# Preparing a selective scan by halves, in another PSUM bank and at another place of a four-layer decoder

## The chip, the cores and the metric

The kernel runs on one core of one Trainium2 chip. The metric is the device time of one execution in microseconds (us). Several executions of the same program are timed, and the median counts. One more execution is recorded by the hardware profiler; all durations of single instructions come from that one.

## The reference, cut to what matters

A decoder of four layers works on `x` of shape (4, 256, 256): 4 sequences of 256 tokens with 256 features. Each layer has an attention, a cross part that takes a context `ctx_1024` of shape (4, 256, 128), and a feed-forward part, each added to `x` and followed by a layer norm. The change touches the first five parts:

- layer 0 attention: 16 query heads of 128 features over one shared key and value head, causal;
- layer 0 cross part: a selective scan over the context, gated by `x`;
- layer 0 feed-forward, the "thought": the last token of each sequence is normed, projected, and put through four rounds of a small network; the result is broadcast to all tokens under a sigmoid gate;
- layer 1 attention: 16 heads of 16 features;
- layer 1 cross part: the same selective scan with other weights.

The scan, with 256 channels `e`, 16 states `n` and 256 positions per sequence:

```python
u = silu(conv4(in_proj_w @ ctx) + conv_b)        # 4 taps along the positions
dt_lo, B, C = split(x_proj_w @ u)                # 8, 16, 16 rows
delta = softplus(dt_proj_w @ dt_lo + dt_proj_b)
state = state * exp(delta * A) + delta * u * B   # one position after the other, A = -exp(A_log)
y = sum_n(state * C) + D * u
out = y * silu(x)
```

`u`, `delta`, `B` and `C` depend on the context alone, not on `x`. So the scan's result is needed only at the gate, after the attention of the same layer.

The thought:

```python
t = norm(x)[:, -1] @ agg
for _ in range(4):
    t = t + gelu(norm(t) @ d1 + d1_b) @ d2 + d2_b
x = norm(x + sigmoid(x @ gate_w + gate_b) * (t @ bc_w + bc_b))
```

## The kernel before, in words

All 1024 tokens stay on the chip: `x` as 8 tiles of 128 tokens, and `xT`, its transpose. The program is emitted in Python and handed to a scheduler that puts the instructions of each engine in an order before the run: an instruction that was emitted earlier has the higher priority, and one emitted later is taken where the engine would stand idle by the scheduler's own clock. [...] Emission order is therefore a priority and not the final order, and a buffer that comes free early lets later work move ahead.

**Scans.** The class `Scans` (from line 398) holds the selective scan. `begin(pre)` starts a generator `_steps`: it first emits the whole preparation for all four sequences and stops. Then each `next` emits one scan, which is one state `n` of one sequence `b`, 64 in a layer. `beside(n)` calls it n times and `upto(b)` until sequence b is done. One scan consists of:

- a DMA on SP that reads rows B and C back from DRAM (`bcd`) to all partitions into a tile `bc` (4 buffers);
- two exponentials on ACT into `dA` (3 tiles), one for each half of the channels;
- a product on POOL, `s = du * B` (4 buffers);
- on DVE the scan itself over 512 columns and the product with C;
- on PE the addition of `s` to the sum over the states, a product with the identity into the PSUM bank `ssmps`. Sequence b keeps that bank from n = 0 to n = 15; there is one such bank.

The preparation uses the same bank for everything: four convolutions of four products each, taps `tap` times context, evicted to `u` on ACT; then for each half of the tokens the product `xp`, whose rows go through `xd` to DRAM, and two products `dt`. Softplus is built from Abs, Exp and Ln on ACT and a sum on DVE (`delta`), and `du = delta * u` is formed on POOL. [...] a change of table is an instruction of its own, ACT_TABLE_LOAD.

**First attention**, `run_mqa` (line 232): 32 items, eight for each sequence, each of four heads and 128 tokens. Item n turns its shares, and beside it the scores of item n + 1, the queries of item n + 4 (in the bank `pm`, tag "mm", one buffer) and two scans are emitted. `gate_pair` for a finished sequence is emitted at the third item of a later sequence. After the last item come the last gate and the preparation of the second layer's scans, `begin("l1x")`.

**Thought**, `run_thought` (line 585): it first centres its weights, then computes the gate (8 tiles, 16 products, one sigmoid over 2048 columns), then takes the last tokens (`last`, `tok`), norms and projects them, and goes through four rounds (`sq`, `var`, `rstd`, `tT`, `h`, `hT`, `add`). After the rounds 24 scans are emitted, and then `gated` and `added` for each sequence, which form the new `x` and its transpose.

**Second attention**, `run_gqa` (line 982) with `SmallHeads`: one scan is emitted beside each of the 8 projections and each of the 32 steps of the heads. `heads16.then` calls `gate_pair` for a sequence whose projection is done. The mixture of experts follows.

Lines 111 (tensor_tensor), 115, 117, 120, 123 (POOL), 126 (ACT) and 132 (PE) are helpers, so in the profile many different operations share one of these lines; the tile's name tells them apart.

Of the kernel before, what the change touches and what calls it, by code (L numbers as in the profile page):

```python
# [19 lines left out]
F32 = mybir.dt.float32  # L20
# [4 lines left out]
AF = mybir.ActivationFunctionType  # L25
# [6 lines left out]
P = 128  # L32
B, L, D = 4, 256, 256
NT = B * L // P
# [197 lines left out]
def run_mqa(K, w, more):  # L232
    nc, tc = K.nc, K.tc
    with ExitStack() as ctx:
# [120 lines left out]
                    K.add_out(2 * b + k, acc[b][:, k, :], not K.fused(0))  # L355

        N = 8 * B
        keys(0)
        queries(0)
        K.scans.begin("l0x")  # L360
# [7 lines left out]
        for n in range(N):  # L368
            shares(n)
            if n + 1 < N:  # L370
                scores(n + 1)
            if n + 4 < N:
                queries(n + 4)
            if n in (2, 3, 4, 5):
                rest.pop(0)()
            if n == 6:
                more()
            K.scans.beside(2)
            turn(n)
            if n:  # L380
                output(n - 1)
            sums(n)
            if n % 8 == 2 and n > 8 and K.fused(0):
                gate_pair(K, wk, y, n // 8 - 1)
        output(N - 1)
        if K.fused(0):
            gate_pair(K, wk, y, B - 1)
            K.scans.begin("l1x")

# [8 lines left out]
class Scans:  # L398
    def __init__(self, K, ctx):
        tc = K.tc  # L400
        self.K = K
        self.one = ctx.enter_context(tc.tile_pool(name="ssm1", bufs=1))
        self.wk = ctx.enter_context(tc.tile_pool(name="ssm2", bufs=4))
        self.ps = ctx.enter_context(tc.tile_pool(name="ssmp", bufs=1, space=PSUM))
        self.dram = ctx.enter_context(tc.tile_pool(name="ssmd", bufs=2, space=bass.MemoryType.DRAM))

        self.dA = [self.one.tile([P, DC, L], F32, name=f"dA{k}") for k in range(3)]
        for t in self.dA:
            K.nc.gpsimd.memset(t[:, :, 0:1], 0.0)
        self.w = {}  # L410
        self.left = iter(())
        self.done = 0

    def load(self, pre):
        K = self.K
# [9 lines left out]

    def begin(self, pre):

        self.left = self._steps(pre)
        self.done = 0
        next(self.left)  # L430

    def beside(self, n):

# [5 lines left out]
        while self.done <= b:  # L439
            next(self.left, None)  # L440

    def _steps(self, pre):
        K, nc, w, wk = self.K, self.K.nc, self.w[pre], self.wk
        cols = w["cols"]
        N = B * L
        u = self.one.tile([P, DC, N], F32, name="u", bufs=2)
        delta = self.one.tile([P, DC, N], F32, name="delta")
        du = self.one.tile([P, DC, N], F32, name="du")


        taps = []
        for j in range(4):
            t = wk.tile([P, D], F32, name="tap", tag="bc", padded_shape=[P, 2 * L])
            nc.sync.dma_start(out=t, in_=K.A[f"{pre}_cw"][:, j * D : (j + 1) * D].to_broadcast([P, D]))
            K.ptt(t, t, w["in"], MUL)
            taps.append(t)
        for h in range(2):
            for c in range(DC):
                ps = self.bank()
                for j in range(4):  # L460
                    K.mm(ps, taps[j][:, c * P : (c + 1) * P], K.ctxp[:, 2 * h : 2 * h + 2, j : j + L], j == 0, j == 3)
                K.act(u[:, c, 512 * h : 512 * h + 512], ps, AF.Identity, bias=cols[:, c, 0:1])
        K.act(u, u, AF.Silu)
        negA = self.one.tile([P, DC, 16], F32, name="negA")
        K.act(negA, cols[:, :, 2:18], AF.Exp)
        K.ts(negA, negA, -1.0, None, MUL)
        bc = self.dram.tile([2, 16, N], F32, name="bcd")
        for h in range(2):
            s = slice(512 * h, 512 * h + 512)
            xd = wk.tile([P, 512], F32, name="xd", tag="s")  # L470
            ps = self.bank()
            for c in range(DC):
                K.mm(ps[0:40, :], w["xp"][:, c, :], u[:, c, s], c == 0, c == DC - 1)
            nc.scalar.copy(xd[0:40, :], ps[0:40, :])
            for k in range(2):
                nc.sync.dma_start(out=bc[k, :, s], in_=xd[8 + 16 * k : 24 + 16 * k, :])
            for c in range(DC):
                ps = self.bank()
                K.mm(ps, w["dt"][:, c * P : (c + 1) * P], xd[0:8, :])

                K.ts(delta[:, c, s], ps, cols[:, c, 1:2], None, ADD)
                K.act(du[:, c, s], ps, AF.Abs, bias=cols[:, c, 1:2])
        K.act(du, du, AF.Exp, scale=-1.0)
        K.act(du, du, AF.Ln, bias=K.eps[1.0])
        for c in range(DC):
            K.stt(delta[:, c, :], delta[:, c, :], 0.0, du[:, c, :], MAX, ADD)
            K.ptt(du[:, c, :], delta[:, c, :], u[:, c, :], MUL)

        turn = 0
        self.y = u  # L490

        late = []
        bank = {}

        def add(b, n, s):
            if n == 0:
                bank[b] = self.bank()
            y = bank[b]
            K.mm(y, K.ident, s.rearrange("p c l -> p (c l)"), n == 0, n == 15)
            if n == 15:  # L500
                for c in range(DC):
                    v = u[:, c, b * L : (b + 1) * L]
                    K.stt(v, v, cols[:, c, 18:19], y[:, c * L : (c + 1) * L], MUL, ADD)
                self.done += 1

        for b in range(B):
            lo = b * L
            for n in range(16):
                yield
                if len(late) > 1:  # L510
                    add(*late.pop(0))
                t = wk.tile([P, 2, L], F32, name="bc", tag="bc")
                nc.sync.dma_start(out=t, in_=bc[:, n, lo : lo + L].unsqueeze(0).to_broadcast([P, 2, L]))
# [14 lines left out]
                K.tt(s, s, again(t[:, 1, :], DC), MUL)  # L528
                late.append((b, n, s))
        for t in late:  # L530
            add(*t)


def gate_pair(K, pool, y, b):

    K.scans.upto(b)
    gate = pool.tile([P, DC, L], F32, name="gate")

    K.act(gate, K.x[:, 2 * b : 2 * b + 2, :], AF.Silu)
# [45 lines left out]
def run_thought(K, w, more):  # L585
# [4 lines left out]
    with ExitStack() as ctx:  # L590
# [79 lines left out]
        cb = one.tile([P, DC], F32, name="cb")  # L670
        nc.vector.tensor_copy(cb, centred(d2b.unsqueeze(2), 1)[:, :, 0])


        gate = one.tile([P, NT, D], F32, name="gate")
        for i in range(NT):
            ps = pm.tile([P, D], F32, name="ps", tag="mm")
            for c in range(DC):
                K.mm(ps, K.xT[:, c, i * P : (i + 1) * P], w["gate"][:, c, :], c == 0, c == DC - 1)
            K.tt(gate[:, i, :], ps, row["gate_b"], ADD)
# [15 lines left out]
        th = one.tile([P, DC, B], F32, name="th")  # L695
        K.tt(th, ps, wide(w["cols"][:, 0, :], B), ADD)
        ct = centred(th, B)

        K.stt(th, wide(d2b, B), 4.0, th, MUL, ADD)
        last = spare.tile([P, B], F32, name="last")  # L700
# [281 lines left out]
def run_gqa(K, w, more):  # L982
    nc, tc = K.nc, K.tc
    more()
    with ExitStack() as ctx:
# [1452 lines left out]
```

## Time and profile before

| | us |
|---|---|
| median of three runs | 2520.05 |
| lowest, highest run | 2504.77, 2521.07 |
| the profiled execution | 2505.99 |
| its span, first to last instruction | 2504.2 |
| mean granted PE clock | 0.939 |
| PE, PEld, DVE, ACT, POOL busy | 2277.2, 1526.3, 1460.8, 802.4, 530.6 |

How to read it: PE is the matrix engine and PEld its weight loads, DVE the vector engine, ACT the scalar engine, POOL the GpSimd, SP the queue that issues DMAs. A float32 product appears as two records[...]. Busy time of PE is modelled and slightly long. Times in the profile count from the first instruction. By the names in the trace the stages end at about 391 us (last item of the first attention), 566 (thought) and 798 (second attention).

### The profile page before, as it was taken

The page shows a single profiled execution, that of the slowest core. Times are in us where ns is not written, and L with a number is a line of the kernel's source. Part 1 is how long each engine was busy: PE and PEld are TensorE (multiplying, and loading weights), DVE is VectorE, ACT ScalarE, POOL GpSimd, SP SyncE. Part 2 cuts the span into 40 slices and gives each one's busy share as a digit, 9 for nine tenths or more (in the row PEclk, how much of TensorE's full clock was granted, in tenths as well). Part 3 has the DMA queues.
Part 4 walks back from the last instruction along what each step waited for, and adds up shares of the span by engine and source line. Part 5 has one row for each costly group of instructions (what it writes and reads, how often), then busy time and mean ns, then how long its engine had stood idle before and what let it go on. Part 6 is the DMA issues. An engine that isn't in the chain of part 4 may idle for free. (4 is left out here: it accounts for less than half of the span.)

```text
span 2504.2 us, 28859 instructions
## 1 busy us (share of the span) xinstructions
PE 2277.2 (91%) x10624; PEld 1526.3 (61%) x10624; DVE 1460.8 (58%) x2824; ACT 802.4 (32%) x1781; POOL 530.6 (21%) x617
## 2 busy tenths in 40 slices
PE   8798988648996999989999999999999989799997
PEld 5466654224443565545888888888776544476774
DVE  3798984588875412182356454444555667774556
ACT  3566663422442111153111111111122244343434
POOL 2544543663332222210001100011110002100001
PEclk9899999677987999999999999999988899999999
DMA  5221221122223254230123111211100002100000
GB/s 197 60 60 45 57 54 40 41 61 42 52 46 109 88 158 130 66 112 29 45 66 110 48 58 45 71 46 47 46 22 1 20 18 70 40 1 1 1 1 17
DMA packets 132836, 138.99 MB, mean 56 GB/s; under 512 B 13876, under 2 KB 120726, under 8 KB 130904
## 3 DMA queue, kind: packets, MB, share of 16 engines
q1 hardware_dynamic: 132696, 137.16, 19.1%
q8 instruction: 84, 1.38, 0.2%
q14 instruction: 56, 0.46, 0.1%
HBM read 134.27 MB, written 2.85 MB: 55 GB/s over the span
## 5 line engine op out<-in xcount | busy, mean ns | idle before, releaser
L132 PE MATMUL ps<-xw,xcT 128*128 128x256 f32 (+1 forms) x2304 | 519.0, 382 | 0.3 <-ACT YT L126 0.3
L132 PEld LDWEIGHTS ps<-xw,xcT 128*128 128x128 f32 x2304 | 430.7, 190 | 64.2 <-issue 1.9
L132 PE MATMUL sc<-kT,qT 32*128 32x256 f32 (+2 forms) x1024 | 240.7, 412 | 11.1 <-DVE qn L129 10.7
L520 DVE TENSOR_TENSOR_SCAN s<-dA,s 128x512 f32<-128x512 f32 x128 | 210.3, 1666 | 35.6 <-POOL s L123 35.4
L123 POOL TENSOR_TENSOR s<-du,bc 128x512 f32<-128x512 f32 x128 | 178.9, 1410 | 231.0 <-PE ssmps L132 191.1
L132 PEld LDWEIGHTS sc<-kT,qT 128*128 128x128 f32 (+1 forms) x1024 | 152.9, 206 | 92.3 <-issue 57.8
L132 PE MATMUL ssmps<-s,idz 128*128 128x512 f32 x256 | 147.1, 683 | 33.6 <-DVE s L111 33.5
L111 DVE TENSOR_TENSOR xp<-ps,xb 128x256 f32<-128x256 f32 x96 | 40.4, 421 | 227.0 <-PE ps L132 224.8
L126 ACT ACTIVATE dA<-delta,negA 128x255 f32<-128x255 f32 x256 | 117.7, 501 | 160.5 <-DVE s L520 160.3
L126 ACT ACTIVATE p<-sc,nm 128x256 f32<-128x256 f32 (+1 forms) x256 | 112.1, 445 | 109.5 <-DVE nm L129 103.7
L111 DVE TENSOR_TENSOR hT<-u,a 128x512 f32<-128x512 f32 x48 | 33.2, 691 | 186.1 <-PE u L132 186.1
L132 PE MATMUL o<-pT,vt 128*128 128x256 f32 (+1 forms) x352 | 121.1, 467 | 21.9 <-ACT pT L332 21.5
L123 POOL TENSOR_TENSOR xp<-xp,rn 128x128 f32<-128x128 f32 x96 | 35.2, 402 | 476.9 <-DVE rn L1406 476.9
L169 POOL TENSOR_SCALAR rstd<-mv 128x2 f32<-128x2 f32 x48 | 12.2, 255 | 551.3 <-DVE mv L161 541.4
L126 ACT ACTIVATE sq<-xp 128x1024 f32<-128x1024 f32 x24 | 25.4, 1057 | 314.3 <-DVE xp L111 314.2
L129 DVE TENSOR_REDUCE qn<-sc 128x2 f32<-128x480 f32 (+1 forms) x192 | 87.2, 506 | 43.6 <-PE sc L132 42.9
L129 DVE TENSOR_REDUCE nm<-sc 128x2 f32<-128x512 f32 (+1 forms) x128 | 77.2, 613 | 49.8 <-PE sc L132 49.2
L126 ACT ACTIVATE e<-sT 128x512 f32<-128x512 f32 x128 | 70.1, 591 | 108.3 <-PE sT L132 107.8
L1474 DVE TENSOR_TENSOR_SCAN dec<-xT,idz 128x256 f32<-128x256 f32 (+1 forms) x192 | 89.8, 537 | 25.0 <-DMA xT<-ad 25.0
L111 DVE TENSOR_TENSOR s<-s,bc 128x512 f32<-128x512 f32 x128 | 103.6, 829 | 1.1
L123 POOL TENSOR_TENSOR hT<-hT,sel 128x512 f32<-128x512 f32 x48 | 60.7, 1268 | 202.1 <-DVE hT L111 102.6
L132 PE MATMUL sT<-q,kT 32*128 32x256 f32 (+1 forms) x384 | 96.4, 502 | 1.7 <-ACT e L126 1.5
(503 smaller groups left out, 4067.1 us busy)
## 6 DMA issues: line engine op xcount, KB each, us to landing
bc<-bcd SPq DMA_DIRECT2D x128, 256.0 KB, 4.6
xw<-in_l2a_xw_dram SPq DMA_DIRECT2D x24, 768.0 KB, 4.9
xT<-ad SPq DMA_DIRECT2D x12, 1024.0 KB, 4.5
wj<-in_l1f_gate_dram SPq DMA_DIRECT2D x48, 128.0 KB, 2.6
wj<-in_l1f_up_dram SPq DMA_DIRECT2D x48, 128.0 KB, 3.1
wj<-in_l1f_down_dram SPq DMA_DIRECT2D x48, 128.0 KB, 3.5
sel<-cwd SPq DMA_DIRECT2D x32, 192.0 KB, 3.0
sel<-cwd SPq DMA_DIRECT2D x32, 128.0 KB, 3.5
```

Source lines behind the costliest of these rows:

```text
L111: self.nc.vector.tensor_tensor(out=out, in0=a, in1=b, op=op)
L123: self.nc.gpsimd.tensor_tensor(out=out, in0=a, in1=b, op=op)
L126: self.nc.scalar.activation(out, in_, func, **kw)
L129: self.nc.vector.tensor_reduce(out=out, in_=in_, axis=AX.X, op=op, **kw)
L132: self.nc.tensor.matmul(out, lhsT=lhsT, rhs=rhs, start=start, stop=stop)
L169: self.nc.gpsimd.tensor_scalar(out=out, in0=in_, scalar1=add, scalar2=None, op0=ADD)
L520: nc.vector.tensor_tensor_scan(out=s.rearrange("p c l -> p (c l)"), data0=dA.rearrange("p c l -> p (c l)"), data1=s.rearrange("p c l -> p ...
L1474: nc.vector.tensor_tensor_scan(out=dec[:, k, h, :], data0=ap[:, h, at(bb, k, j) : at(bb, k, 2)], data1=K.idz[:, 0 : (2 - j) * P], initial=0.0,
```

## The change: what it does

- `begin` is split into `prepare(pre, bank)`, a generator that emits the preparation into banks that the caller hands in, and `start(pre)`, which sets up the scans. `start` no longer takes the generator's first `next`, so the first call of `beside` counts one step that emits no scan.
- The preparation goes by halves of two sequences: `u`, `delta` and `du` are tiles of one half with three buffers each (before: whole tiles, `u` with two buffers, the others with one). Within a half it runs from the convolutions to `du`. Silu reads PSUM directly. The taps have tiles of their own. `du` is formed on DVE.
- For the second layer it is emitted behind the last gate of the first attention as before, now with products into `pm`, the bank of the queries, and eight scans are emitted right after it.
- Gates of the first attention are emitted three items later, and `gate_pair` no longer calls `upto` itself; its callers do, or have emitted enough.
- In the thought the last tokens' path comes ahead of the gate's 16 products, and 32 scans are emitted in place of 24.

```diff
@@ run_mqa
+        bank = lambda: pm.tile([P, 512], F32, name="ps", tag="mm")
...
-            if n % 8 == 2 and n > 8 and K.fused(0):
-                gate_pair(K, wk, y, n // 8 - 1)
+            if K.fused(0):
+                if n % 8 == 5 and n > 8:
+                    gate_pair(K, wk, y, n // 8 - 1)
         output(N - 1)
         if K.fused(0):
+            K.scans.upto(B - 1)
             gate_pair(K, wk, y, B - 1)
-            K.scans.begin("l1x")
+            for _ in K.scans.prepare("l1x", bank):
+                pass
+            K.scans.start("l1x")
+            K.scans.beside(8)
@@ class Scans
     def begin(self, pre):
-        self.left = self._steps(pre)
+        for _ in self.prepare(pre, self.bank):
+            pass
+        self.start(pre)
+
+    def start(self, pre):
+        self.left = self._steps(*self.ready[pre])
+        halves = self.ready[pre][1]
+        self.y = lambda b: halves[b // 2][0][:, :, b % 2 * L : b % 2 * L + L]
         self.done = 0
-        next(self.left)
...
-    def _steps(self, pre):
+    def prepare(self, pre, bank):
...
-        u = self.one.tile([P, DC, N], F32, name="u", bufs=2)
-        delta = self.one.tile([P, DC, N], F32, name="delta")
-        du = self.one.tile([P, DC, N], F32, name="du")
...
-            t = wk.tile([P, D], F32, name="tap", tag="bc", padded_shape=[P, 2 * L])
+            t = self.one.tile([P, D], F32, name=f"tap{j}")
...
         for h in range(2):
+            u, delta, du = (self.one.tile([P, DC, 2 * L], F32, name=n, bufs=3) for n in ("u", "delta", "du"))
+            halves.append((u, delta, du))
             for c in range(DC):
-                ps = self.bank()
+                ps = bank()
                 for j in range(4):
                     K.mm(ps, taps[j][:, c * P : (c + 1) * P], K.ctxp[:, 2 * h : 2 * h + 2, j : j + L], j == 0, j == 3)
-                K.act(u[:, c, 512 * h : 512 * h + 512], ps, AF.Identity, bias=cols[:, c, 0:1])
-        K.act(u, u, AF.Silu)
+                K.act(u[:, c, :], ps, AF.Silu, bias=cols[:, c, 0:1])
...
-        K.act(du, du, AF.Exp, scale=-1.0)
-        K.act(du, du, AF.Ln, bias=K.eps[1.0])
-        for c in range(DC):
-            K.stt(delta[:, c, :], delta[:, c, :], 0.0, du[:, c, :], MAX, ADD)
-            K.ptt(du[:, c, :], delta[:, c, :], u[:, c, :], MUL)
+            K.act(du, du, AF.Exp, scale=-1.0)
+            K.act(du, du, AF.Ln, bias=K.eps[1.0])
+            yield
+            for c in range(DC):
+                K.stt(delta[:, c, :], delta[:, c, :], 0.0, du[:, c, :], MAX, ADD)
+                K.tt(du[:, c, :], delta[:, c, :], u[:, c, :], MUL)
+                yield
+
+    def _steps(self, cols, halves, negA, bc):
...
@@ gate_pair
-    K.scans.upto(b)
...
-    K.ptt(gate, gate, y[:, :, b * L : (b + 1) * L], MUL)
+    K.ptt(gate, gate, y(b), MUL)
@@ run_thought
-        gate = one.tile([P, NT, D], F32, name="gate")
-        for i in range(NT):
...
-        K.act(gate, gate, AF.Sigmoid)
         last = K.tp.tile([B, D], F32, name="last", tag="tp")
...
         ct = centred(th, B)
+        gate = one.tile([P, NT, D], F32, name="gate")
+        for i in range(NT):
...
+        K.act(gate, gate, AF.Sigmoid)
...
-        K.scans.beside(24)
+        K.scans.beside(32)
@@ run_gqa
-            heads16.then = lambda b: gate_pair(K, wk, K.scans.y, b)
+            def then(b):
+                K.scans.upto(b)
+                gate_pair(K, wk, K.scans.y, b)
+            heads16.then = then
```

More of the change, by code (lines that the diff above doesn't have):

```diff
@@ L412, in __init__ @@
         self.done = 0
+        self.ready = {}
     def load(self, pre):
@@ L440, in upto @@
             next(self.left, None)
-    def _steps(self, pre):
+    def prepare(self, pre, bank):
         K, nc, w, wk = self.K, self.K.nc, self.w[pre], self.wk
         cols = w["cols"]
-        N = B * L
-        u = self.one.tile([P, DC, N], F32, name="u", bufs=2)
-        delta = self.one.tile([P, DC, N], F32, name="delta")
-        du = self.one.tile([P, DC, N], F32, name="du")
+        negA = self.one.tile([P, DC, 16], F32, name="negA", bufs=2)
+        bc = self.dram.tile([2, 16, B * L], F32, name="bcd")
+        halves = []
+        self.ready[pre] = cols, halves, negA, bc
         taps = []
         for j in range(4):
-            t = wk.tile([P, D], F32, name="tap", tag="bc", padded_shape=[P, 2 * L])
+            t = self.one.tile([P, D], F32, name=f"tap{j}")
             nc.sync.dma_start(out=t, in_=K.A[f"{pre}_cw"][:, j * D : (j + 1) * D].to_broadcast([P, D]))
@@ L456, in _steps @@
             taps.append(t)
+        yield
+        K.act(negA, cols[:, :, 2:18], AF.Exp)
+        K.ts(negA, negA, -1.0, None, MUL)
         for h in range(2):
+            u, delta, du = (self.one.tile([P, DC, 2 * L], F32, name=n, bufs=3) for n in ("u", "delta", "du"))
+            halves.append((u, delta, du))
             for c in range(DC):
-                ps = self.bank()
+                ps = bank()
                 for j in range(4):
                     K.mm(ps, taps[j][:, c * P : (c + 1) * P], K.ctxp[:, 2 * h : 2 * h + 2, j : j + L], j == 0, j == 3)
-                K.act(u[:, c, 512 * h : 512 * h + 512], ps, AF.Identity, bias=cols[:, c, 0:1])
@@ L463, in _steps @@
-        K.act(u, u, AF.Silu)
[L464 to L469, printed above, removed]
+                K.act(u[:, c, :], ps, AF.Silu, bias=cols[:, c, 0:1])
+            yield
             xd = wk.tile([P, 512], F32, name="xd", tag="s")
-            ps = self.bank()
+            ps = bank()
@@ L472, in _steps @@
             for c in range(DC):
-                K.mm(ps[0:40, :], w["xp"][:, c, :], u[:, c, s], c == 0, c == DC - 1)
+                K.mm(ps[0:40, :], w["xp"][:, c, :], u[:, c, :], c == 0, c == DC - 1)
             nc.scalar.copy(xd[0:40, :], ps[0:40, :])
             for k in range(2):
-                nc.sync.dma_start(out=bc[k, :, s], in_=xd[8 + 16 * k : 24 + 16 * k, :])
+                nc.sync.dma_start(out=bc[k, :, 2 * h * L : 2 * h * L + 2 * L], in_=xd[8 + 16 * k : 24 + 16 * k, :])
+            yield
@@ L477, in _steps @@
             for c in range(DC):
-                ps = self.bank()
+                ps = bank()
                 K.mm(ps, w["dt"][:, c * P : (c + 1) * P], xd[0:8, :])
-                K.ts(delta[:, c, s], ps, cols[:, c, 1:2], None, ADD)
-                K.act(du[:, c, s], ps, AF.Abs, bias=cols[:, c, 1:2])
-        K.act(du, du, AF.Exp, scale=-1.0)
-        K.act(du, du, AF.Ln, bias=K.eps[1.0])
-        for c in range(DC):
-            K.stt(delta[:, c, :], delta[:, c, :], 0.0, du[:, c, :], MAX, ADD)
-            K.ptt(du[:, c, :], delta[:, c, :], u[:, c, :], MUL)
+                K.ts(delta[:, c, :], ps, cols[:, c, 1:2], None, ADD)
@@ new lines, in prepare @@
+                K.act(du[:, c, :], ps, AF.Abs, bias=cols[:, c, 1:2])
+            yield
+            K.act(du, du, AF.Exp, scale=-1.0)
+            K.act(du, du, AF.Ln, bias=K.eps[1.0])
+            yield
+            for c in range(DC):
+                K.stt(delta[:, c, :], delta[:, c, :], 0.0, du[:, c, :], MAX, ADD)
+                K.tt(du[:, c, :], delta[:, c, :], u[:, c, :], MUL)
+                yield
+    def _steps(self, cols, halves, negA, bc):
+        K, nc, wk = self.K, self.K.nc, self.wk
@@ L489, in _steps @@
         turn = 0
-        self.y = u
         late = []
@@ L501, in add @@
                 for c in range(DC):
-                    v = u[:, c, b * L : (b + 1) * L]
+                    lo = b % 2 * L
+                    v = halves[b // 2][0][:, c, lo : lo + L]
                     K.stt(v, v, cols[:, c, 18:19], y[:, c * L : (c + 1) * L], MUL, ADD)
@@ L506, in _steps @@
         for b in range(B):
-            lo = b * L
+            lo = b % 2 * L
             for n in range(16):
                 yield
+                _, delta, du = halves[b // 2]
                 if len(late) > 1:
@@ L512, in _steps @@
                 t = wk.tile([P, 2, L], F32, name="bc", tag="bc")
-                nc.sync.dma_start(out=t, in_=bc[:, n, lo : lo + L].unsqueeze(0).to_broadcast([P, 2, L]))
+                nc.sync.dma_start(out=t, in_=bc[:, n, b * L : b * L + L].unsqueeze(0).to_broadcast([P, 2, L]))
                 dA = self.dA[turn % 3]
@@ L671, in run_thought @@
         nc.vector.tensor_copy(cb, centred(d2b.unsqueeze(2), 1)[:, :, 0])
-        gate = one.tile([P, NT, D], F32, name="gate")
-        for i in range(NT):
[L676 to L679, printed above, removed]
-        K.act(gate, gate, AF.Sigmoid)
         last = K.tp.tile([B, D], F32, name="last", tag="tp")
@@ L697, in run_thought @@
         ct = centred(th, B)
+        gate = one.tile([P, NT, D], F32, name="gate")
+        for i in range(NT):
+            ps = pm.tile([P, D], F32, name="ps", tag="mm")
+            for c in range(DC):
+                K.mm(ps, K.xT[:, c, i * P : (i + 1) * P], w["gate"][:, c, :], c == 0, c == DC - 1)
+            K.tt(gate[:, i, :], ps, row["gate_b"], ADD)
+        K.act(gate, gate, AF.Sigmoid)
         K.stt(th, wide(d2b, B), 4.0, th, MUL, ADD)
@@ L1032, in run_gqa @@
         if K.fused(3):
-            heads16.then = lambda b: gate_pair(K, wk, K.scans.y, b)
+            def then(b):
+                K.scans.upto(b)
+                gate_pair(K, wk, K.scans.y, b)
+            heads16.then = then
         heads16.run(ctx, lambda: K.scans.beside(1))
```

## The prediction

> **What bounds the kernel now.** I read the page's 40 slices first, then a table of busy time by stretch, then what each engine waited for inside a stretch, last the instructions in order of time around the places that the diff touches. The chain of waits on the page follows back only to 2065 us and says nothing of the first 800, where the change lies.
>
> The slices are 62.6 us each. The change touches slices 1 to 13: first attention to 391 us, thought (the first feed-forward part) to 566, second attention to about 798.
>
> ```profile
> PE   8798988648996999989999999999999989799997
> DVE  3798984588875412182356454444555667774556
> ```
>
> PE and DVE are both nearly full in the first attention, PE alone in the second, and neither at 375 to 563. The table by stretch (columns: length, then busy time and count of PE, PEld, DVE, ACT, POOL, then PE clock, DMA share, GB/s) says it in numbers:
>
> ```profile
> 320.00:371.00 51.00, 41.93 (x176) 28.54 (x175) 42.90 (x60) 31.11 (x89) 22.58 (x18) 0.93 0.19 52
> 371.00:391.00 20.00, 16.92 (x61) 10.35 (x62) 9.83 (x15) 9.63 (x26) 5.35 (x6) 1.00 0.12 27
> 391.00:423.00 32.00, 27.26 (x94) 14.46 (x94) 13.05 (x25) 13.27 (x20) 12.97 (x27) 0.89 0.09 31
> 423.00:463.00 40.00, 29.18 (x112) 14.09 (x110) 10.47 (x24) 19.70 (x26) 16.16 (x21) 0.70 0.14 30
> 463.00:500.00 37.00, 22.52 (x116) 9.77 (x116) 30.02 (x27) 16.59 (x33) 24.84 (x16) 0.78 0.29 68
> 500.00:527.00 27.00, 18.89 (x71) 8.44 (x70) 24.88 (x27) 12.23 (x25) 15.12 (x10) 0.81 0.38 87
> 527.00:566.00 39.00, 12.20 (x30) 5.25 (x28) 33.69 (x73) 4.21 (x9) 25.86 (x30) 0.64 0.18 39
> 660.00:710.00 50.00, 48.38 (x314) 23.11 (x312) 41.75 (x60) 22.76 (x44) 14.81 (x14) 0.86 0.23 50
> ```
>
> From 391 to 463 DVE works 23.5 of 72 us; from 463 to 566 it works 88.6 of 103 and is the bound. The same table for the scans' tile s alone shows why: no scan runs in those 72 us.
>
> ```profile
> 391.00:463.00 72.00, 0.00 (x0) 0.00 (x0) 0.00 (x0) 0.00 (x0) 0.78 0.12 30
> ```
>
> The next lines in order of time show what holds the second layer's scans back. The bank ssmps is let go by the last scan of the first layer at 386.70, the preparation's first product enters it at 390.82, and its ten uses of one bank end only with du at 450; the first scan's POOL product comes at 466.06. In the same time the thought's own chain waits: its input xT is whole at 413.4 (copy at 412.78), but tok is copied at 431.77, behind the 16 gate products in PE's queue.
>
> ```profile
> 386.70 0.87 DVE L120 SCALAR_TENSOR_TENSOR u<-u,w_l0x_cols,ssmps 128x256 f32<-128x256 f32 x2 [3.15 <-PE ssmps L132]
> 390.82 1.02 PE L132 MATMUL ssmps<-ctxp,tap 128*128 128x512 f32 x2
> 431.77 0.40 DVE L686 COPY tok<-last 4x256 f32<-4x256 f32 x1
> 466.06 4.64 POOL L123 TENSOR_TENSOR s<-du,bc 128x512 f32<-128x512 f32 x3
> ```
>
> In the second attention, 610 to 700, the waits of PE have one line, 2.6 us in 90: PE is the bound there, and its 40 scans' additions are part of it.
>
> ```profile
> PE sc L132 <- DVE qn L129: 2.6, 4, 1.2
> ```
>
> [...] a scan takes 1185 ns at least and 2298 at most, its POOL product 1257 to 2263. [...] all s rows on DVE are 309.7 us over 128 scans, 2.42 us. [...] The trace has 63 loads of 1283; [...] so I use 1.28. [...]
>
> **The change part by part.**
>
> *Thought.* The preparation of the second layer uses the queries' bank, free once the last rotated query is read (about 353 us); its taps have own buffers, so their four SP loads no longer stand in the scans' bc ring (before, they took SP from 371.8 to 383.9); its four bcd writes go out on SP as before, and 15 bc reads with their scans move ahead on SP and POOL, which work 15 to 25 us of each stretch here. It is 16 convolution products, 4 of xp, 4 of dt: 48 passes of PE records at 0.43 us spacing, 20.6 us. Its bank chain is 4 x 4.4 (from the first layer's evictions at 39.1 to 52.5) + 2 x 2.9 + 4 x 2.9 = 35 us, so from 353 it can end near 390 to 400. Scans can then follow the first layer's last one, near 391 instead of 466. Eight are asked for before the thought and 32 in it, the first call only starting the generator: 39 instead of 24 done at its end. DVE now works 13.05 + 10.47 + 30.02 + 24.88 + 33.69 = 112.1 us from 391 to 566, 66.0 of it scans, so 46 other. Then 46 + 39 x 2.42 = 140; at the density of 500:527 (24.88 / 27 = 0.92) that is 152 us, end at 543 instead of 566: -23. The chain permits this: with tok before the gate products it can start at 414 instead of 432, the four rounds last 17 to 21 us each beside scans (sq at 482.15, then 499.00), so it ends at about 492 and the gated part follows the scans. Its gain of 18 is not added; DVE is the later of the two. Against it: the layer norm and gate chain of 393 to 413 has some eight hops on DVE and POOL, and each may now stand behind a scan. I take **-20**, between -35 (DVE filled before 391 too) and -5 (scans start at 420).
>
> *Second attention.* 25 scans instead of 40 are left. One addition costs two passes; the spacing to the next product is 0.96 to 1.06 us at the granted 0.77 to 0.90. 15 x 1.04 = **-15**, as PE does not wait there. Bounds: -22 (DVE's 36 us less there also removes the waits of 745 to 770), and -3 if the attention's own exponentials, two of 0.59 us after each pair of products, pace it once the fill is gone. The tail from 783 to 800 (reciprocal, projection, norm, gate) is no scan's and stays.
>
> *First attention.* The first layer by halves: half 0 needs two convolutions (8.9), xp and two dt (9), Exp, Ln, sum and product (6) and table loads: 27 to 30 us after 35.1, so scans can start at about 65 instead of 87.3. Four s buffers hold them until half 1 leaves the bank (about 78): three or four scans, 7 to 10 us of DVE's work, move into a stretch where DVE is busy 31.8 of 83. PE, the other bound, does the same work: I take -4. Ahead of it stand Silu straight from PSUM and Exp, Ln per half: four to eight more table loads per layer, 5 to 10 us of ACT, beside its 35% free time, but PE's largest wait of 94 to 371 is on ACT's pT (17.3 us). du's product goes from POOL (2 x 2.8) to DVE (4 x 0.68, the nearest row is s<-s,bc). The l1x products now take 20.6 us of PE before about 395, where 320 to 391 has 12 us free; the rest lengthens it or displaces idle waits: +4, from -8 to +25 for the stage. Sum **0**. Gate pairs three steps later: same instructions, nothing, give or take 2.
>
> Sum: -20 - 15 + 0 = -35. The profiled execution took 2505.99 (span 2504.2), so 2471 in its own time; the median of the three runs is 2520.05, 14 above it, and by that measure I state 2520 - 35 = **2485**.
>
> **The rivals.** *More overlap* (0.17): the first attention gives 8 and thought 30, attention 20: 2462. For it: DVE's empty 391 to 463[...]. *Only the second attention gains* (0.14): hops behind scans and a late preparation cost the thought what the scans win: 2520 - 15 = 2505. *The scans' place is not what paces the second attention* (0.07): thought -20, attention -3: 2497. *Slower* (0.07): the preparation, planned into PE's and ACT's idle slots, lands in the last attention's queues. All 20.6 us of PE and ten table loads (12.8) displace pT copies, 33; the first layer's eight loads add 10; the thought's PSUM, which reuses the queries' bank, waits until the preparation leaves it, and the scans then hold its chain, so the thought gains nothing: +43 - 15 = +28, 2548. It decides once the stage ends more than 35 us later than 391.
>
> **How the numbers follow.** The forecast itself has 0.55. About 1% (25 us) is what a measurement of this kernel can tell from no change, since its three runs differ by 0.65%. Of the forecast's 0.55 I count 0.50 beyond 25 us and 0.05 within. Faster 0.50 + 0.17 = 0.67; within 0.05 + 0.14 + 0.07 = 0.26; slower 0.07. The range goes from 2450, a little under the rival with more overlap, to 2515, above the case of attention alone; it leaves out the slower one and little else.
>
> **What would show it.** Right: s rows on DVE from about 395 on; the first l1x convolution near 355; tok near 415; the thought's last xT copy near 545; 25 scans after it; no s row in the last 16 steps of the second attention; MoE's first g product at about 785 instead of 819. Wrong: convolutions after 390; acc's last addition past 400; PE waiting on exponentials in the second attention; DVE waiting for POOL or bc in the thought.

## The result and the profile after

The changed kernel took 2520.8 us (median of 22 runs) beside 2512.7 for the kernel before (22 runs): ratio 1.0037, 95% interval 1.002 to 1.0055 (the ratios here are taken over the runs; the quotient of these two medians is 1.0032). The forecast was 2485, so the sign was wrong. The profiled execution has a span of 2523.4 us (before: 2504.2).

PE and DVE in the 40 slices, from the page of the kernel after:

```profile
PE   8898987766997899989999999999999989799997
DVE  4888975788673512173346454444555667774456
```

Slice 8, inside the thought, has 7 on DVE where it had 5. Slices 11 and 13, in the second attention, have 6 and 3 where they had 8 and 5, and PE is about as full there as before. The table by stretch is plainer (columns: length, then busy time and count of PE, PEld, DVE, ACT, POOL, then PE clock, DMA share, GB/s):

```profile
384.00:401.00 17.00, 12.42 (x34) 4.62 (x32) 8.44 (x20) 5.33 (x9) 9.66 (x19) 0.90 0.16 55
401.00:433.00 32.00, 22.75 (x39) 7.78 (x38) 17.79 (x23) 23.01 (x36) 8.14 (x8) 0.75 0.24 58
433.00:449.00 16.00, 11.67 (x53) 6.50 (x52) 15.67 (x17) 10.20 (x16) 7.08 (x5) 0.82 0.34 72
449.00:500.00 51.00, 36.02 (x132) 19.41 (x132) 33.90 (x42) 20.52 (x37) 32.21 (x30) 0.68 0.28 58
500.00:552.00 52.00, 35.10 (x155) 13.67 (x153) 46.51 (x43) 23.72 (x49) 29.62 (x20) 0.84 0.38 90
552.00:590.00 38.00, 15.76 (x42) 8.93 (x43) 31.79 (x80) 5.70 (x12) 24.95 (x37) 0.61 0.13 31
```

and the same for the tile s alone (busy time and count of PE, PEld, DVE, POOL; one scan is two rows on DVE):

```profile
384.00:401.00 17.00, 0.43 (x2) 0.00 (x0) 0.00 (x0) 0.00 (x0) 0.90 0.16 55
401.00:433.00 32.00, 4.30 (x6) 1.47 (x6) 10.43 (x8) 7.36 (x6) 0.75 0.24 58
433.00:449.00 16.00, 6.32 (x10) 1.72 (x8) 13.21 (x10) 7.08 (x5) 0.82 0.34 72
```

No scan runs on DVE to 401 us and few to 433. From 433 to 590 DVE is busy 127.9 of 157 us: the scans did fill it, as forecast, but the stage did not end sooner for it. The instructions around the change, in order of time, first three of the kernel before and then those of the changed one:

```profile
393.69 0.76 DVE L111 TENSOR_TENSOR x<-acc,x 128x256 f32<-128x256 f32 x2 [6.12 <-PE acc L132]
568.73 0.59 ACT L100 COPY xT<-ps 128x512 f32<-128x512 f32 x1 [1.64 <-PE ps L187]
819.37 2.07 PE L132 MATMUL g<-xT,wj 128*128 128x512 f32 x2 [0.68 <-ACT rows L100]
```

```profile
382.75 0.76 DVE L111 TENSOR_TENSOR x<-acc,x 128x256 f32<-128x256 f32 x2 [4.54 <-PE acc L132]
384.27 2.31 PE L132 MATMUL ps<-ctxp,tap 128*128 128x512 f32 x5
401.46 0.41 DVE L701 COPY tok<-last 4x256 f32<-4x256 f32 x1 [2.92 <-PE last L699]
416.42 2.51 POOL L123 TENSOR_TENSOR s<-du,bc 128x512 f32<-128x512 f32 x2 [12.94 <-DVE du L111]
432.13 0.67 ACT L126 ACTIVATE du<-ps,w_l1x_cols 128x512 f32<-128x512 f32 x1
434.86 0.59 PE L132 MATMUL ps<-w_d1b,idz 128*128 128x256 f32 x2
448.86 0.18 ACT L126 ACTIVATE sq<-ps 128x8 f32<-128x8 f32 x1 [0.90 <-PE ps L132]
589.28 0.59 ACT L100 COPY xT<-ps 128x512 f32<-128x512 f32 x1 [1.59 <-PE ps L187]
836.58 1.99 PE L132 MATMUL g<-xT,wj 128*128 128x512 f32 x4 [0.68 <-ACT rows L100]
```

These are the marks of the stages used below. The first attention ends at 382.8 (before 393.7). The preparation's convolutions begin at 384.3, not at 355. The last tokens are there at 401.5 (before 431.8), yet the first product into the thought's own PSUM pool (its set of banks), w_d1b, waits until the preparation's last eviction, du, has left the queries' bank (432.8). So the first round starts at 448.9, later than before (438.1). The thought's last xT copy comes at 589.3 (before 568.7), the first product of the mixture of experts at 836.6 (before 819.4).

A second profile of the same kernel (after_again) has these marks at 382.4, 446.8, 586.1 and 831.5. Differences under some 3 us in the thought and 5 us at the end of the second attention are therefore not read as effects.

### The profile page after: what moved, and what is told of

Its sections match the earlier page's. It is cut to its first block, busy times and chain, and to the rows that moved or that the text cites. A ratio compares the mean times of both kernels' runs of the same rounds, so it can differ in the third digit from the quotient of the medians.

```text
span 2523.4 us, 28881 instructions
## 1 busy us (share of the span) xinstructions
PE 2294.8 (91%) x10624; PEld 1534.0 (61%) x10624; DVE 1469.8 (58%) x2836; ACT 814.3 (32%) x1794; POOL 518.4 (21%) x613
## 5 line engine op out<-in xcount | busy, mean ns | idle before, releaser
L123 POOL TENSOR_TENSOR s<-du,bc 128x512 f32<-128x512 f32 x128 | 176.0, 1389 | 249.9 <-PE ssmps L132 194.3
L132 PE MATMUL ssmps<-s,idz 128*128 128x512 f32 x256 | 152.5, 707 | 55.6 <-DVE s L111 37.9
L126 ACT ACTIVATE dA<-delta,negA 128x255 f32<-128x255 f32 x256 | 116.9, 501 | 148.9 <-DVE s L544 148.7
L132 PEld LDWEIGHTS ssmps<-s,idz 128*128 128x128 f32 x256 | 49.6, 214 | 103.3 <-DVE s L111 52.8
```

Of the source, the lines that this page charges most:

```text
L123: self.nc.gpsimd.tensor_tensor(out=out, in0=a, in1=b, op=op)
L126: self.nc.scalar.activation(out, in_, func, **kw)
L132: self.nc.tensor.matmul(out, lhsT=lhsT, rhs=rhs, start=start, stop=stop)
```

## The experiments

Theories and rivals are called by the letters that the expectations give them. All marks are from one profile of each kernel; "thought" is from the last addition of acc to the last xT copy, "second attention" from there to the first g product. "Scans inside" counts the second layer's scans that stand in DVE's own list of instructions ahead of the thought's last addition.

| kernel | scans inside | acc | last xT | thought | second attention | first g | ratio to before (95%) |
|---|---|---|---|---|---|---|---|
| before | 24 | 393.7 | 568.7 | 175.0 | 250.6 | 819.4 | 1 |
| after | 40 | 382.8 | 589.3 | 206.5 | 247.3 | 836.6 | 1.0037 (1.002-1.0055) |
| after_again | 40 | 382.4 | 586.1 | 203.7 | 245.4 | 831.5 | one execution |
| e1_queries_bank_apart | 39 | 383.3 | 590.2 | 206.9 | 246.3 | 836.5 | 1.0056 (1.0033-1.0079) |
| e2_scans_bank | 39 | 383.5 | 593.8 | 210.3 | 249.2 | 843.0 | 1.0065 (1.0048-1.0082) |
| e3_gate_first | 40 | 383.4 | 584.1 | 200.7 | 245.4 | 829.4 | 1.0009 (0.9991-1.0026) |
| e4_24_scans | 40 | 381.2 | 585.6 | 204.4 | 237.9 | 823.5 | 1.0043 (1.0023-1.0062) |
| p1_early_preparation | 44 | 405.6 | 594.1 | 188.5 | 241.1 | 835.2 | 1.0036 (1.0017-1.0056) |
| h2_no_scan_in_thought | 0 | 385.5 | 522.1 | 136.7 | 308.6 | 830.7 | 1.003 (1.0009-1.005) |
| gates3_cap16 | 16 | 385.4 | 542.5 | 157.2 | 267.3 | 809.9 | 0.995 (0.9929-0.997) |
| cap24 | 24 | 382.9 | 557.1 | 174.2 | 249.9 | 807.0 | 0.9957 (0.9941-0.9973) |
| halves_alone | 26 | 391.0 | 560.5 | 169.6 | 247.2 | 807.7 | 0.9966 (0.9945-0.9987) |
| gates3_new_scans | 26 | 382.9 | 555.7 | 172.8 | 251.3 | 807.0 | 0.9949 (0.9934-0.9965) |
| before_gates3 | 24 | 389.8 | 564.5 | 174.7 | 254.4 | 818.9 | 0.9985 (0.9966-1.0005) |
| e1_cap24 | 24 | 383.5 | 548.0 | 164.6 | 256.1 | 804.1 | 0.9951 (0.9931-0.9971) |
| e3_cap24 | 24 | 384.9 | 557.3 | 172.4 | 249.6 | 806.8 | 0.998 (0.9956-1.0004) |
| e1_e3_cap24 | 24 | 383.6 | 548.5 | 164.9 | 256.3 | 804.8 | 0.9955 (0.9936-0.9974) |

### First theory: the thought waits for the queries' bank

```diff
@@ e1_queries_bank_apart, run_mqa
+        pm = ctx.enter_context(tc.tile_pool(name="mqapm", bufs=1, space=PSUM))
         ctx.enter_context(K.turns())
-        pm = ctx.enter_context(tc.tile_pool(name="mqapm", bufs=1, space=PSUM))
@@ e2_scans_bank, run_mqa
-            for _ in K.scans.prepare("l1x", bank):
+            for _ in K.scans.prepare("l1x", K.scans.bank):
```

> The changed kernel (2520.8 us) with one edit: the queries' pool pm is opened ahead of the turning pool tp in the first attention, so its bank becomes bank 6, and the thought's pool thp (banks 2 to 4) no longer lies over it. Theory A (the thought's PSUM pool waits until the preparation has left the queries' bank): the w_d1b product comes near 400 us instead of 434.9, the first sq near 425 instead of 448.9, the thought's last xT copy near 570 instead of 588, and the time falls by 10 to 25 us against the changed kernel, to 2496 to 2511. Rival B (the 40 scans beside the chain stretch it, and DVE sets the thought's end): sq comes early but the four rounds stretch from 103 to 115 us or more, the last xT copy stays past 583, and the time is within 5 us of 2521.

> The changed kernel with the bank part of the change undone: the preparation of l1x goes into the scans' own bank ssmps again. Theory A: the thought's pool is free at once, as in the kernel of e1, so the w_d1b product comes near 400 us and the time falls by 10 to 25 us against the changed kernel; the first scans of l1x start no later (about 416 us), since the bank is only needed two scans later for their sum. Rival B: within 5 us of 2521. Were the scans' bank needed for the overlap, the first s on POOL would come after 435 and the time would be above 2521.

Order of time in e1_queries_bank_apart:

```profile
401.00 0.70 PE L132 MATMUL ps<-w_d1b,idz 128*128 128x256 f32 x2 [0.73 <-ACT xT L100]
413.67 0.18 ACT L126 ACTIVATE sq<-ps 128x8 f32<-128x8 f32 x1 [1.07 <-PE ps L132]
590.19 0.56 ACT L100 COPY xT<-ps 128x512 f32<-128x512 f32 x1
```

The wait is real and the edit removes it: w_d1b runs at 401.0 and the first round starts 35 us earlier. Nothing is gained. From the first sq to the mean after the rounds (lastmean) it takes 122.7 us where after takes 103.1, and from there to the last xT copy 53.9 instead of 37.3. Both kernels were expected at 2496 to 2511 by theory A and measured 2526.7 and 2526.8, slightly above after. In e2 the first sq comes at 415.5 and the last xT copy at 593.8, the same picture. Theory A fell as an explanation of the loss. Rival B (DVE and the scans) held in its marks; its time, within 5 us of 2521, was missed by under 1 us.

### Other parts undone

```diff
@@ e3_gate_first: the block "gate = ... AF.Sigmoid" stands ahead of "last = K.tp.tile(...)" again
@@ e4_24_scans
-            K.scans.beside(8)
+            K.scans.beside(0)
...
-        K.scans.beside(32)
+        K.scans.beside(25)
```

> The changed kernel with one part undone: the thought's gate block (16 products, sums, sigmoid) stands ahead of the last tokens' path again. Theory A: the block waits for the same pool, so it runs from 435 to 447 and pushes agg and ct behind it; first sq within 5 us of 449, last xT copy within 5 of 588, time within 8 us of 2521. Rival C (the moved gate block with its sigmoid and POOL products inside the first round is what slows the rounds): the rounds shrink from 103 by 10 or more and the time falls by 8 us or more.

> The changed kernel with the number of scans undone: none asked for ahead of the thought and 24 in it, as before the change (40 are left for the second attention). Theory A: the w_d1b product stays at 435 us, the rounds fall from 103 to about 82 to 90, the thought's last xT copy comes near 565 to 570 instead of 588, but the second attention takes 15 additions more, 13 to 16 us[...]; time within 8 us of 2521. Rival B (the scans' place is the loss, as they gain nothing in the second attention[...]): thought -20, second attention +2, time near 2503.

e3_gate_first is 2513.3 us, ratio 1.0009; its interval overlaps that of after a little, and its marks are within some 2 us of after_again's. Its rounds do shrink, from 103 to 90 us, as rival C had it, but the first sq comes 7 us later than in after (455.8). It may be worth some us; it is not settled. e4_24_scans did not do what it was meant to, and told the most of the four: DVE's list still holds 40 scans inside the thought. Once the preparation is early, scans emitted later fill the same places, and "40 emitted" decides nothing. Its early second attention (237.9 us) did not show in the time, 1.0043: from the first g product to the end its profile takes 1693.6 us, where after takes 1686.8. Why is left open.

### The number of scans inside the thought

To set that number I used a data dependency. negA is multiplied by a column made from the x that the thought has finished, so later exponentials wait for it:

```diff
@@ cap24, end of run_thought (beside(0) and beside(25) as in e4)
             added(b, *this)
+        hold = one.tile([P, 1], F32, name="hold")
+        K.ts(hold, K.x[:, NT - 1, 0:1], 0.0, 1.0, MUL, ADD)
+        negA = K.scans.ready["l1x"][2]
+        K.ts(negA, negA, hold, None, MUL)
@@ h2_no_scan_in_thought: the same with -1.0, negA's own factor -1 left out for l1x,
   no beside ahead of it, more of them in the second attention
```

> The changed kernel with the second layer's scans held back until the thought has ended: their factor negA is multiplied by -1 only there, from a column of the last x. The list of DVE then has 0 of them ahead of the thought's last addition (24 in the kernel before, 40 in the changed one and also in e4_24_scans), and all 64 stand beside the second attention. Theory D (the number of scans that DVE takes inside the thought sets its end, at 1.2 us each over before, while the second attention pays only some 0.2 us for each): the thought's last xT copy near 550 to 558 instead of 589, the second attention longer by 10 to 25 us since DVE is then full there (150 of 241 us plus 39 x 2.5), and the time 10 to 20 us under the changed kernel. Rival E (a scan costs the same at either place): the end of the second attention stays at 836 within 5 us. Rival F (the chain, not DVE, sets the thought): last xT copy past 575, time above the changed kernel's by 15 us or more.

> The changed kernel with the 25th and all later scans of the second layer held until the thought's last x is there (negA is multiplied by 1 from a column of x at that point); the first 24 may start as early as in the changed kernel. Preparation, banks, gate block and the first attention's gates stay as changed. DVE's list has 24 scans ahead of the thought's last addition instead of 40. Theory D (the scans cost the thought 1.6 to 1.9 us each, by 0 scans: 137 us, 24: 175, 40: 206, while the second attention takes up to some 40 for nearly nothing): last xT copy near 560 instead of 586 to 589, second attention 247 to 252 us as in the kernel before, its end near 810, and the time 15 to 25 us under the changed kernel, 2495 to 2505. Rival E (a scan costs the same wherever it stands): thought 25 us shorter, second attention 25 us longer, time within 5 us of the changed kernel. Rival A (the queries' bank and the moved gate block are the loss): w_d1b still at 434, time within 5 us of the changed kernel.

The table by stretch from the end of the first attention to that of the thought, in h2_no_scan_in_thought, cap24 and after:

```profile
385.00:522.00 137.00, 89.24 (x373) 49.06 (x371) 46.69 (x135) 37.37 (x55) 47.81 (x77) 0.68 0.06 17
```

```profile
383.00:557.00 174.00, 109.22 (x418) 51.89 (x416) 109.18 (x185) 67.13 (x110) 88.34 (x101) 0.77 0.21 49
```

```profile
383.00:589.00 206.00, 133.71 (x450) 60.94 (x449) 154.10 (x221) 87.88 (x153) 110.86 (x116) 0.75 0.27 62
```

Without scans the thought needs 137 us and 46.7 of DVE, the 46 of my prediction. With 24 scans it needs 174 and 109.2, with 40 it needs 206 and 154.1. Sixteen scans more are 44.9 us of DVE and 32.3 us of the stage (29.5 by after_again): 1.8 to 2.0 us each. Even the first 24 cost 37.5, 1.6 each. With the queries' bank apart the price is higher: 39 scans instead of 24 (e1_queries_bank_apart and e1_cap24) are 42.3 us, 2.8 each. The preparation stands inside this stage in all of these kernels.

The second attention goes 247.3 or 245.4 (24 scans), 249.9 (40), 267.3 (48), 308.6 (64): it takes 40 for little and pays 2.2 to 2.6 us for each beyond. One profile says no more than that of the difference from 24 to 40, since kernels with 24 or 25 scans there lie between 237.9 and 249.2 us and those with 38 or 40 between 247.2 and 256.3; the means of the two groups are 6.7 us apart, some 0.4 us for each scan.

The kernel cap24, which differs from e4_24_scans by the hold alone, is about 20 us faster than e4_24_scans and after (0.9957 against 1.0043 and 1.0037). So the number of scans inside the thought is the cause of the loss against that kernel. Theory D held on cap24. On h2 it failed: its 1.2 us for a scan in the thought was too low and its 0.2 us in the second attention was wrong far beyond 40. The mark of 830.7 is 6 us under after's 836.6, and rival E, which allowed 5, came nearer.

The third round of the thought shows how the price arises, first DVE in after, then in h2_no_scan_in_thought:

```profile
505.44 4.42 DVE L544 TENSOR_TENSOR_SCAN s<-dA,s 128x512 f32<-128x512 f32 x2 [1.16 <-ACT dA L126]
509.77 0.66 DVE L111 TENSOR_TENSOR s<-s,bc 128x512 f32<-128x512 f32 x1
510.36 0.15 DVE L115 TENSOR_SCALAR rstd<-ps 128x4 f32<-128x4 f32 x1
510.43 0.68 DVE L111 TENSOR_TENSOR s<-s,bc 128x512 f32<-128x512 f32 x1
512.01 0.17 DVE L111 TENSOR_TENSOR tT<-ps,rstd 128x8 f32<-128x8 f32 x1 [0.90 <-POOL rstd L123]
512.09 0.16 DVE L111 TENSOR_TENSOR cs<-ps,cb 128x8 f32<-128x8 f32 x1
```

```profile
471.83 0.16 DVE L115 TENSOR_SCALAR rstd<-ps 128x4 f32<-128x4 f32 x1 [8.36 <-PE ps L132]
473.11 0.17 DVE L111 TENSOR_TENSOR tT<-ps,rstd 128x8 f32<-128x8 f32 x1 [1.12 <-POOL rstd L123]
473.19 0.16 DVE L111 TENSOR_TENSOR cs<-ps,cb 128x8 f32<-128x8 f32 x1
```

The round's sq is on ACT at 506.26 in after and at 470.55 in h2. rstd follows on DVE 4.1 us later in after, behind two scans and a product, and 1.28 us later in h2. Then ACT has two exponentials of the scans and a change of table ahead of h. ACT in after, then in h2:

```profile
506.26 0.18 ACT L126 ACTIVATE sq<-ps 128x8 f32<-128x8 f32 x1 [0.81 <-PE ps L132]
514.39 0.91 ACT L126 ACTIVATE dA<-delta,negA 128x255 f32<-128x255 f32 x2 [3.60 <-DVE s L544]
515.31 1.28 ACT L126 ACT_TABLE_LOAD   x1
516.61 0.38 ACT L126 ACTIVATE h<-ps 128x256 f32<-128x256 f32 x1
```

```profile
470.55 0.18 ACT L126 ACTIVATE sq<-ps 128x8 f32<-128x8 f32 x1 [1.17 <-PE ps L132]
475.35 0.38 ACT L126 ACTIVATE h<-ps 128x256 f32<-128x256 f32 x1 [4.62 <-PE ps L132]
```

So h comes 10.35 us after sq in after and 4.80 in h2, which has no table load in its last three rounds. Of the 5.55 us between them 2.8 are the wait on DVE, 1.28 the table and 0.9 the two exponentials. The four rounds are 17.1, 14.5, 10.0 and 10.5 us in h2; in after they are 36.6, 20.8, 21.7 and 24.1. How the price divides among the engines in the other rounds is not worked out.

> The kernel of gates3_new_scans with only 16 scans allowed in the thought, the other 48 held until its last x. Theory D: the thought is 10 x 1.6 = 16 us shorter than with 26, and the second attention takes 48 scans: if it is full at 40, each of the 8 to 10 more costs it up to 2.4 us (40 scans: 250 us, 64: 309), so +0 to +24, and the time lies within 10 us of gates3_new_scans on either side. Rival (the second attention still has room at 48): time 10 to 16 us under gates3_new_scans.

gates3_cap16 adds the same hold, and beside(17), to gates3_new_scans below. 16 scans instead of 26 give the thought 15.6 us, and the second attention takes 16.0 more: the ratio is the same, 0.995 and 0.9949, as theory D had left room for. Past 40 the two stages only trade.

### Where the preparation stands

```diff
@@ p1_early_preparation, run_mqa's loop
+                if n == N - 4:
+                    prep = K.scans.prepare("l1x", bank)
+                for _ in range(3 if n >= N - 4 else 0):
+                    next(prep)
```

> The changed kernel with the preparation of l1x emitted in pieces beside the last four items of the first attention (the queries' bank is free by then), where my prediction had put it. Theory D: first convolution near 340 to 360 us, first POOL s of l1x near 390 to 400 instead of 416, DVE's empty time from 384 to 433 fills with some 8 scans, w_d1b near 400, and the thought's end comes 10 to 20 us earlier; the first attention pays 0 to 15 us for 20 us of products. Time 0 to 15 us under the changed kernel. Rival G (every product and table load brought into the first attention lengthens it by its own time): last acc addition near 405 instead of 383, thought's end unchanged, time within 5 us of the changed kernel or above.

```profile
353.93 3.60 PE L132 MATMUL ps<-ctxp,tap 128*128 128x512 f32 x8
405.62 0.74 DVE L111 TENSOR_TENSOR x<-acc,x 128x256 f32<-128x256 f32 x2
```

This puts the convolutions where I had predicted them, at 354. The first attention ends 22.9 us later, the preparation's whole 20.6 us of products and a little more; the thought is 18 us shorter and ends at 594, 5 us after the changed kernel's 589. Rival G held, with its time: 1.0036 is what after has. Theory D failed here: it had the thought's end 10 to 20 us earlier, and 0 to 15 us for the first attention. The thought is shorter although 44 scans stand in it, so the preparation's place there costs time too: moved into the first attention, it costs that stage 22.9 us and takes 18 from the thought.

### What gave the first attention its 11 us

```diff
@@ halves_alone = after with e2, e3 and e4 together, and
-                if n % 8 == 5 and n > 8:
+                if n % 8 == 2 and n > 8:
@@ gates3_new_scans = halves_alone with n % 8 == 5;  before_gates3 = before with n % 8 == 5
```

> The new Scans class (preparation by halves, Silu from PSUM, du on DVE) with the rest of the change undone: the scans' own bank for l1x too, no scans ahead of the thought and 24 in it, the gate block first, the gates of the first attention three items earlier. DVE's list has 26 scans ahead of the thought's last addition (24 before the change). Theory D: the first attention keeps its 11 us (last acc addition near 383), the thought takes no more than before (about 175 to 180 us), the time is 5 to 12 us under the kernel before. Rival H[...]: the stages' marks come 11 us earlier, but the time is within 3 us of before.

> The kernel of halves_alone with the first attention's gates emitted at the sixth item of a sequence (as changed) instead of the third; 26 scans in the thought by DVE's list. If the 11 us of the first attention (last acc addition at 383 instead of 391 to 394) come from the gates' place, they come back here: last acc addition near 383, thought's end near 552, second attention's end near 800, and the time 5 to 10 us under halves_alone (2501), near 2493. If they come from elsewhere (the queries' bank for the preparation), the marks stay those of halves_alone: 391, 560, 808.

> The kernel before with one edit: the first attention's gates stand three items later. Theory: the last acc addition comes near 383 instead of 394, as in the changed kernel, so that the gates' place and not the halves give the first attention its gain; the rest as before: time 5 to 11 us under the kernel before. Rival (the halves give it: scans start at 66 us instead of 87): last acc addition stays at 391 to 394, time within 3 us of before.

The last addition of acc comes at 391.0 with the halves alone, 389.8 with the later gates alone and 382.9 with both (393.7 before). Neither rival was right: each gives 3 to 4 us, together 11. The small gains are from one profile each and no larger than the 4 us by which this mark moves among the kernels that share the changed first attention (381.2 to 385.5), so only the gain of both together is clear. halves_alone (0.9966) and gates3_new_scans (0.9949) are both faster than before, and their intervals overlap; before_gates3 is not told from before. The two faster ones have 26 scans in the thought: the new class is good, and the loss lies in what the change does with it afterwards.

### The first theory once more, with the scans capped

> The kernel of cap24 with the queries' bank apart from the thought's pool (the edit of e1). If the wait for the bank was covered by DVE's scans, it shows now: w_d1b near 401 instead of 435.6, first sq near 414 instead of 444.5, and the thought's last xT copy 10 us or more ahead of cap24's 557, the time 5 to 15 us under cap24 (ratio to before 0.990 to 0.994 where cap24 has 0.9957). If the wait costs nothing, because the 24 scans and the preparation fill the same time anyhow: last xT copy within 5 us of 557, ratio within 0.2% of 0.9957.

> The kernel of cap24 with the gate block ahead of the last tokens' path again (the edit of e3). If the moved gate block costs the chain its time: last xT copy about 5 us ahead of 557, ratio to before about 0.993 to 0.995. If its gain in e3 came only with the full DVE: last xT copy within 2 us of 557, ratio within 0.2% of 0.9957.

> Both edits on cap24: queries' bank apart and gate block first. If the two add up: last xT copy near 540 to 545 and ratio to before 0.989 to 0.993, the fastest of all; if they cover each other or cost nothing: like the better of e1_cap24 and e3_cap24, and like gates3_new_scans (0.9949).

The edits of e1 and e3 on cap24. With DVE less full (109.2 of 174 us in cap24, 154.1 of 206 in after), the bank apart does bring the thought's end forward, 548.0 instead of 557.1, where it brought nothing with 40 scans: the wait had been covered. The second attention then takes 6 us more, and the ratios (0.9951, 0.998, 0.9955) are not told from cap24's 0.9957. The gains in time that the expectations gave for the case that the wait or the gate block costs something (0.990 to 0.994, 0.993 to 0.995, and 0.989 to 0.993 for both) did not come. The moved gate block moves no mark of the table here. The fastest versions, gates3_new_scans, gates3_cap16, e1_cap24, e1_e3_cap24 and cap24, lie within 0.1% of one another, 11 to 13 us under the kernel before and 20 to 22 under the changed one.

## Why the prediction was wrong

The rival named Slower had the closest mechanism, but its point of decision, a first attention that ends over 35 us late, was not what decided.

- *Thought, -20; measured +31.5 (by after_again +28.7).* This is the step that failed: "46 + 39 x 2.42 = 140; at the density of 500:527 (24.88 / 27 = 0.92) that is 152 us". The count was right (40 scans for 39, 46.7 us of other work on DVE for 46), and DVE's total was a tenth too low (140 us forecast, 154 measured). The length, forecast 152 us and measured 206, was wrong for two reasons. The sum began at 391 at full density, while DVE worked 26.2 of the 49 us from 384 to 433, since the convolutions came at 384 and the first scan's product on POOL at 416. The bank was free by 354, where p1 puts them; why they were not moved forward in the changed kernel stays open. And I took DVE's idle time in the thought for room, because the rounds "last 17 to 21 us each beside scans" in the trace of before. Those rounds were already stretched: from sq to sq they take 20.0, 24.0, 16.9 and, to lastmean, 20.6 us, so the reading left out the 24.0; bare ones take 10 to 17. The scans are not filler there, they stand in the chain's queues.
- *Chain start, tok at 415 and free to go on.* tok came at 401.5, but the first round at 448.9. The pool wait was in my rivals at 0.07 and true; e1 shows that removing it alone gives nothing.
- *Second attention, -15; measured -3.3 (-5.2).* The term 15 x 1.04 was mis-sized: it took the PE time of the additions as time gained. The table from the last xT copy to the first exponential, and from there to the last one, in before and in after:

```profile
569.00:623.00 54.00, 48.83 (x189) 27.00 (x189) 45.05 (x89) 13.09 (x36) 20.18 (x38) 0.78 0.23 49
623.00:779.00 156.00, 145.50 (x902) 65.53 (x899) 120.75 (x172) 68.15 (x130) 49.67 (x45) 0.88 0.21 45
```

```profile
589.00:648.00 59.00, 53.94 (x190) 30.31 (x189) 43.67 (x86) 12.06 (x33) 19.08 (x38) 0.73 0.17 41
648.00:797.00 149.00, 140.85 (x875) 64.27 (x871) 91.58 (x142) 55.66 (x100) 28.73 (x30) 0.85 0.09 20
```

  The heads do shorten, from 155.7 to 148.9 us, 0.4 us for each of the 16 scans gone, at a clock of 0.85 instead of 0.88. The additions did go as priced: in these stretches their PE time is 25.1 us instead of 40.2. But the heads' own products got longer, above all those into o, from 414 to 460 ns with ones and from 379 to 418 ns with vt. That is 10 to 11%, where the clock of these stretches fell by 3 to 4%; what lengthened them is not shown. The bound of -3 that I gave for exponentials that pace the stage was met in number only: PE waits for e for 2.5 us of the 149 (0.6 before). The projections before the heads take 59 us instead of 54, at 0.73 instead of 0.78; gates3_new_scans passes them in 55 us at 0.72. The lower clock goes with these losses in both profiles of after, but it is not shown to be their cause, which stays open.
- *First attention, 0; measured -11.* Halves and later gates were taken as -4 and nothing; together they gave 11, below my bound of -8. The +4 for the preparation's products did not occur because they ran behind the attention; p1 shows they would have cost 23, inside my upper bound of 25.
- *The sum.* -11 + 31.5 - 3.3 = +17 at the first g product, which after_again puts at +12. The ratio says +9 (5 to 14). From that mark to the span's end the profiles take 1684.8 (before), 1686.8 (after) and 1676.4 us (after_again), so the rest can lie in stages that the change does not touch. The starting point of the forecast, 2520, was the median of three runs; 22 runs gave 2512.7.
- *The price of a scan.* I priced a scan at the mean of its s rows on DVE in before, 2.42 us. DVE's s rows in the thought of cap24 are 63.06 us for 24 scans, 2.63 us each, so the price was near and a little low. What spreads the scan instruction from 1185 to 2298 ns in before is not shown by any run here.

## What to carry to other kernels

Idle time on an engine inside a latency-bound chain (a stage of short steps, each of which waits for the one before it) was not free room here: background instructions delayed the next step that was queued behind them, by 2.8 us on DVE in the round shown. A scan cost the stage 1.6 to 2.8 us, while a PE-bound stage took 40 of the same at some 0.4 us each. Before moving work, run the stage once without it; the bare length (137 us against 175) says what the background already costs. And limit background work by a dependency rather than by emission order, since the scheduler here filled idle slots with whatever was ready (e4_24_scans).

## What the runs showed of the hardware that was not expected

- Background exponentials on ACT brought table loads of 1.28 us into a chain whose last three rounds had none without them (h2_no_scan_in_thought). In the round of after that is shown, one stands at 515.31 us between the exponentials and h, and one at 517.01 between h and the next exponential. The first is 1.28 of the 5.55 us by which sq to h is longer.
- The same kernel's marks moved by 3 us in the thought and 5 us at the second attention's end between two profiled executions, and its span by 15 us (2523.4 and 2507.9), 10 of these 15 us behind the first g product, in stages far from the change.
- A background scan cost DVE 2.63 us inside the thought of cap24 but 60.45 us / 30 = 2.0 us in the second attention of before, by that profile's s rows from 623 to 779 us. Why is not shown.
